# The output projection of a chunk in two halves of eight heads, and the last four heads of the last chunk as a chain by halves of tokens

## The chip, the core and the metric

The kernel runs on one core of a Trainium2 chip. The core has a matrix engine (TensorE, PE in the profile; its weight loads are shown as PEld), a vector engine (VectorE, DVE), an activation engine (ScalarE, ACT), a general engine (GpSimd, POOL) and SyncE (SP), which here only issues transfers. Matmuls write into PSUM, a memory of banks of 512 float32 columns by 128 partitions; VectorE and ScalarE read it from there. The metric is the time of one execution on the device, in microseconds.

## What is computed

Two transformer layers on `x` of 2 sequences by 1024 tokens by 256 features. In each layer attention and feed-forward both read the same normalised input and both are added to the residual. The parts that matter here belong to the second layer:

```python
# _L1_attn_ref: 16 heads of 16 features, rotary positions
attn = jnp.einsum('bhqd,bhkd->bhqk', q, k) * scaling
probs = jax.nn.softmax(attn, axis=-1)
out = jnp.einsum('bhqk,bhkd->bhqd', probs, v)
out = out.transpose(0, 2, 1, 3).reshape(B, S, D)
return out @ out_w.T + out_b
...
xn = _layernorm(x, axis=-1)
x = x + _L1_attn_ref(xn, ...) + _L1_ffn_ref(xn, ...)
return x
```

`out @ out_w.T` is a sum over 256 features, so over 16 heads. It can be cut by heads: the product of the features of heads 0 to 7 with their rows of `out_w.T`, plus that of heads 8 to 15.

## The kernel before

The 2048 tokens are four chunks of 512 (`C`); a chunk is four blocks of 128 tokens (`CT`). `xc[c]` is the residual of chunk `c`, and everything is added into it by VectorE. `parts_left[c]` counts what is still to be added to a chunk: two feed-forward blocks (of 256 tokens, `F`) and the projection. Whoever brings it to zero sends the chunk out.

Layer 0 is ordered by a planner with listed due times (`LEADS`); the change does not touch it. Layer 1 is ordered by hand. Its attention works in eight **units**, each four heads of one sequence: four units for sequence 0, four for sequence 1. A unit has two passes over chunks (`n` = 0, 1), and each pass 8 steps over blocks of 128 keys. The loop at L1332 to L1357 runs over units 0 to 6, 16 steps each. In a step TensorE makes scores for the next unit's maxima (`scm`, read by VectorE's reduction `peak`), scores for this unit's weights (`sce`, read by ScalarE's exponential `pr`), and the weighted sums of the step before (`weigh`, into the bank `po`). The last unit has its own loop (L1360 to L1368) without `scm`.

Between these, TensorE is given **filler** work: a list of generators (the feed-forward blocks of layer 1, `ffn1`, and others). A generator yields the cost of the matmuls it has just issued. `slot` (L1322) shares what is left over the slots left, `left[0] / to_fill[0]`, and lets `fill` (L1216) run the list until that share is spent. In the last unit a slot counts one half. A generator that yields `SOON` has a result on the way which another engine must fetch. There `fill` stops, unless at least 0.85 us (`LEAD`) are still owed; then the next step comes at `go_on(SOON, FIRST)`, in the middle of the next step of the unit, behind the first peak reduction. Units that begin with `heads_of` (L1341) also run an `urgent` list in each slot, whose time is taken off the filler's share.

When a pass has its eighth step, `weigh` copies `po` to `oT` (512 tokens by 4 heads) and asks for `normalise` two slots later (L1131 to L1134). `normalise` transposes `oT` block by block, takes the reciprocal of the sums and multiplies into `att`, the tile of the chunk's 256 features. After the last of the four units of a sequence (`g == NG - 1`, L1151) it queues `project` behind the filler that is running (`queue_next`, L1199). `project` (L1156) transposes all of `att`, four transposes for each half `k` of the features into a bank each, copies one bank by ScalarE and the other by VectorE into `aT`, and then, for each of four token blocks, makes a sum of two products (`mm`), adds it to `xc[c]` and, if this completes the chunk, sends the 128 tokens out. The order of the end (L1369 to L1373) is: the last `weigh`, and then all that is due or left in the filler.

Banks named by `bank(...)` come from one ring of three; `po` has a bank of its own; `sce` and `scm` come from a ring of two pairs. `aT` comes from a ring of three tiles named "stage", which the loads of layer 1's weights also use.

Of the kernel before, what the change touches and what calls it, by code (L numbers as in the profile page):

```python
# [13 lines left out]
F32 = mybir.dt.float32  # L14
# [7 lines left out]
P = 128  # L22
B, S, D = 2, 1024, 256
NH, HD = 16, 16
E = 1024
NB = E // P
C = 512
NC = B * S // C
CT = C // P
BT = S // P  # L30
F = 256
HS = 32
VW = HD + 1
NG = 4
# [5 lines left out]
COL = 4 / 2400  # L40
PASS = 1.1 / 2400
TR = 2 / 2400
# [316 lines left out]
def tile_two_layers(ctx: ExitStack, tc: tile.TileContext, a: dict, out: bass.AP):  # L359
    nc = tc.nc  # L360
    x_d = a["x"].rearrange("(t p) d -> p t d", p=P)
    out_d = out.rearrange("(t p) d -> p t d", p=P)

    state = State()
    tensor, vector, scalar, gpsimd, sync = (
        Engine(state, which, getattr(nc, n))
        for which, n in ((PE, "tensor"), (DVE, "vector"), (ACT, "scalar"), (POOL, "gpsimd"), (None, "sync"))
    )

    def open_pool(stack, name, bufs, grain=1, **kw):  # L370
        return Pool(state, stack.enter_context(tc.tile_pool(name=name, bufs=bufs, **kw)), bufs, grain)

    const = open_pool(ctx, "const", 1)
    small = open_pool(ctx, "small", 4)
    ps = open_pool(ctx, "ps", 1, 2 * C, space=PSUM)
    ident = const.tile([P, P], F32, tag="ident", name="ident")
# [6 lines left out]
    def bank(name):  # L383
        return ps.tile([P, C], F32, tag="bank", name=name, bufs=3)

    po = ps.tile([P, C], F32, tag="po", name="po", bufs=1)
# [16 lines left out]
    def load_w(pool, name, k, n, tag=None):  # L403

        return load(pool, name, a[name].rearrange("(k p) n -> p k n", p=P), [P, k // P, n], tag)
# [6 lines left out]
    xc, xnT = [], []  # L412
# [23 lines left out]
    def mm(out_, pairs):  # L436
        for i, (lhsT, rhs) in enumerate(pairs):
            tensor.matmul(out_, lhsT=lhsT, rhs=rhs, start=(i == 0), stop=(i == len(pairs) - 1))
# [4 lines left out]
    SOON, FIRST, SECOND, LAST, PAIR = 1, 2, 3, 4, 5  # L443
# [102 lines left out]
    def run(gen):  # L546
        for _ in gen:
            pass
# [5 lines left out]
    at = open_pool(ctx, "at", 2)  # L554
# [34 lines left out]
    wo1 = load_w(const, "woT1", D, D)  # L589
# [413 lines left out]
        yield from hadamard_in("wuT1", "wB")  # L1003


    parts_left = [C // F + 1] * NC

    def part_done(c):
        parts_left[c] -= 1
# [16 lines left out]
    units = [(b, g) for b in range(B) for g in range(NG)]  # L1026
# [6 lines left out]
    def later(slots, f):  # L1033
        due.append([slots, f])

    def tick():
        for d in due:
            d[0] -= 1
        ready = [d for d in due if d[0] <= 0]
        due[:] = [d for d in due if d[0] > 0]  # L1040
        for _, f in ready:
            f()
# [76 lines left out]
    att = {}  # L1119

    def weigh(u, n, kt, pr):
        b, g = units[u]
        for h in range(4):
            tensor.matmul(
                po[h * HS : h * HS + VW, :],
                lhsT=va[b, g][:, kt, h, :],
                rhs=pr[h // 2][:, h % 2, :],
                start=(kt == 0),
                stop=(kt == BT - 1),
            )  # L1130
        if kt == BT - 1:  # L1131
            oT = late[0].tile([P, C], F32, tag="oT", name="oT", bufs=1)
            vector.tensor_copy(oT, po)
            later(2, lambda: normalise(u, n, oT))  # L1134

    def normalise(u, n, oT):
        b, g = units[u]
        pt = bank("pt")
        for j in range(CT):
            tensor.transpose(pt[:, j * P : (j + 1) * P], oT[:, j * P : (j + 1) * P], ident)  # L1140
        p4 = pt.rearrange("p (t h s) -> p t h s", t=CT, h=4)
        rz = small.tile([P, CT, 4], F32, tag="rz1", name="rz1")
        vector.reciprocal(rz, p4[:, :, :, HD])
        if g == 0:
            att[b, n] = late[0].tile([P, CT, D], F32, tag="att", name="att")
        vector.tensor_mul(
            att[b, n][:, :, g * 4 * HD : (g + 1) * 4 * HD].rearrange("p t (h d) -> p t h d", h=4),
            p4[:, :, :, 0:HD],
            rz.unsqueeze(3).to_broadcast([P, CT, 4, HD]),
        )  # L1150
        if g == NG - 1:  # L1151
            later(1, lambda: queue_next(project(b, n)))
        left[0] -= CT * P * TR
        spent[0] += CT * P * TR

    def project(b, n):  # L1156

        c = b * (NC // B) + n
        aT = at.tile([P, 2, C], F32, tag="stage", name="aT", bufs=3)
        pts = []  # L1160
        for k in range(2):
            pts.append(bank("pt"))
            for j in range(CT):
                tensor.transpose(pts[k][:, j * P : (j + 1) * P], att[b, n][:, j, k * P : (k + 1) * P], ident)
        yield 2 * CT * P * TR, SOON
        scalar.copy(aT[:, 0, :], pts[0])
        vector.tensor_copy(aT[:, 1, :], pts[1])
        yield 0.0
        parts_left[c] -= 1
        last = parts_left[c] == 0  # L1170
        for j in range(CT):
            py = bank("py")[:, 0:D]
            mm(py, [(aT[:, k, j * P : (j + 1) * P], wo1[:, k, :]) for k in range(2)])
            yield 2 * D * COL, SOON
            vector.tensor_add(xc[c][:, j, :], py, xc[c][:, j, :])
            if last:
                sync.dma_start(out=out_d[:, c * CT + j, :], in_=xc[c][:, j, :])
            yield 0.0

    def search(part):  # L1180

        for i in range(STEPS // 4):
            j = part // 2 * 16 + part % 2 * 2 + i // 2 * 4 + i % 2
            sc = pair("sc")
            plan.burst = True
            burst(scores_of(0, j, sc))
            plan.burst = False
            scores_max(0, j, sc)
            yield
# [9 lines left out]
    def queue_next(gen):  # L1199

        filler.insert(1, gen) if filler else filler.append(gen)

    def step(queue, k=0):
        if callable(queue[0]):
            background.append(queue.pop(0)())
            return
        try:
            x = next(queue[0])
        except StopIteration:
            queue.pop(0)  # L1210
            return
        waits[queue[0]] = x[1] if isinstance(x, tuple) else 0
        spent[k] += cost_of(x)
        left[0] -= cost_of(x)
# [31 lines left out]
    def force(queue):  # L1246
        while queue:
            if queue is background:
                run(queue.pop(0))
            else:  # L1250
                step(queue)
# [16 lines left out]
    halves = norm_halves(xc[0], xnT[0])  # L1268
# [51 lines left out]
    pending = []  # L1320
# [8 lines left out]
    def keep(u, i, prs):  # L1329
        pending.append((u, i // 16, i % 16 // 2, prs))  # L1330
# [28 lines left out]
    u = len(units) - 1  # L1359
    for i in range(0, STEPS, 2):  # L1360
        scs = [pair("sce") for _ in range(2)]
        burst([x for p in range(2) for x in weights_of(u, i, p, scs[p])])
        prs = [weights_exp(sc) for sc in scs]
        go_on(SOON, FIRST)
        while pending:
            weigh(*pending.pop(0))
        slot(0.5)
        keep(u, i, prs)  # L1368
    while pending:  # L1369
        weigh(*pending.pop(0))  # L1370
    while due or filler:
        tick()
        force(filler)  # L1373


def _constants():
# [64 lines left out]
```

## Time and profile before

| | us |
|---|---|
| three runs | 898.34, 898.73, 900.73 (median 898.73) |
| the profiled execution | 900.66 |
| its span, first to last instruction | 898.9 |
| granted TensorE clock, mean | 0.996 of full |
| first half of the program, layer 0 and the first maxima | up to about 203 |
| units 0 to 6 | to about 836 |
| last unit | to 888.9 |
| from the end of `po` to the end | 888.9 to 898.9 |

A row of the timeline gives the start in us, the duration in us, the engine, the operation, the tile written and the tiles read, the shapes, how many instructions are merged, and in brackets how long the engine was idle before and who ended that. All rows have line 316, where a helper issues them, so one goes by tile names. A float32 matmul of the program shows as two rows, and a transpose as one. A matmul's end is modelled, so the start of the next reader is the better mark. The costliest groups that the change's neighbours belong to:

| group | rows | mean ns | engine |
|---|---|---|---|
| `pr<-sce` 128x1024, exponential | 256 | 1023 | ACT |
| `peak<-scm`, reduction | 224 | 1223 | DVE |
| `x<-py` 128x256, add from PSUM | 64 | 419 | DVE |
| `oT<-po` 128x512, copy | 16 | 686 | DVE |
| `aT<-pt` 128x512, copy | 4 | 586 | ACT |
| `aT<-pt` 128x512, copy | 4 | 689 | DVE |
| `va<-pkv` 128x256, copy from PSUM | 16 | 367 | ACT |
| `va<-pqkv` 128x128, add from PSUM | 32 | 281 | DVE |
| `rz<-pt` 128x16, reciprocal | 16 | 250 | DVE |

`out` is written in 16 transfers of 128 KB, with 1.7 us from issue to landing as the median.

### The profile page before, as it was taken

The numbers are of one execution on the slowest core, as the hardware profiler recorded it, in microseconds if no ns is written. First come the engines' busy times: TensorE is split into PE (matmuls) and PEld (weight loads), VectorE is DVE, ScalarE is ACT, GpSimd is POOL, SyncE is SP. The second block draws the span as 40 slices with busy tenths as digits, with TensorE's granted clock in tenths as the row PEclk, the third lists the DMA queues.
The fourth block names the chain that finished last, engine by engine and source line by source line (L and its number), as shares of the span: only waits on it lengthen the run. The fifth ranks groups of instructions, "written<-read, shape, count | busy, mean of one in ns | idle before, by whom it ended". The sixth has DMA issues, their size and how long they took to land.

```text
span 898.9 us, 14598 instructions
## 1 busy us (share of the span) xinstructions
PE 864.9 (96%) x6064; PEld 518.0 (58%) x6064; DVE 583.0 (65%) x956; ACT 438.4 (49%) x641; POOL 212.6 (24%) x280
## 2 busy tenths in 40 slices
PE   8999999989999989999999999999999999999997
PEld 5699866675566434555555555555555555555533
DVE  5887567887677785656865656677565655656211
ACT  6646464515566443445544444455444444444563
POOL 2656877404452140015300000153000000000000
PEclk9999999999999999999999999999999999999999
DMA  9200000000010110000000000000000000000001
GB/s 308 76 1 1 1 1 1 1 1 1 2 48 1 47 47 1 1 1 1 1 1 1 1 1 24 1 1 2 24 1 1 1 1 1 1 1 1 1 7 41
DMA packets 11313, 14.77 MB, mean 16 GB/s; under 512 B 1264, under 2 KB 8944, under 8 KB 11248
## 3 DMA queue, kind: packets, MB, share of 16 engines
q1 hardware_dynamic: 11248, 13.85, 4.6%
q8 instruction: 47, 0.77, 0.4%
q14 instruction: 18, 0.15, 0.1%
HBM read 11.75 MB, written 2.10 MB: 15 GB/s over the span
## 4 chain that ended last, share of the span: by engine, by line
PE 72%; DVE 22%; ACT 3%; issue 2%; DMA 1%; POOL 0%; SPq 0%; ACTq 0%; DVEq 0%
PE pug L316 19%; DVE peak L316 17%; PE scm L316 16%; PE py L316 13%; PE sce L316 7%; PE pqkv L316 5%; PE pt L316 4%; PE pw L316 2%; PE po L316 2%; PE pkv L316 1%; PE sc L316 1%; PE pq L316 1%; ACT pr L316 1%; DVE att L316 1%; DVE t_wgT L316 1%
## 5 line engine op out<-in xcount | busy, mean ns | idle before, releaser
L316 ACT ACTIVATE pr<-sce 128x1024 f32<-128x1024 f32 x256 | 260.2, 1023 | 269.4 <-PE sce L316 269.0
L316 DVE TENSOR_REDUCE peak<-scm 128x2 f32<-128x1024 f32 x224 | 274.0, 1223 | 167.7 <-PE scm L316 167.0
L316 PE MATMUL po<-pr,va 128*17 128x512 f32 x1024 | 135.6, 598 | 0.0
L316 PEld LDWEIGHTS scm<-qk_hi 32*128 32x128 f32 x448 | 41.5, 182 | 151.1 <-DVE peak L316 113.6
L316 PE MATMUL sce<-qk_hi 32*128 32x512 f32 x512 | 123.0, 495 | 4.8 <-DVE peak L316 2.4
L316 PE MATMUL scm<-qk_hi 32*128 32x512 f32 x448 | 111.8, 495 | 11.7 <-DVE peak L316 1.0
L316 POOL CAST tops<-nm 128x16 fp32r<-128x16 f32 x16 | 3.4, 211 | 404.8 <-DVE nm L316 402.3
L316 PE MATMUL sce<-mx,ones_r 32*128 32x512 f32 x512 | 97.3, 392 | 0.1
L316 PE MATMUL sce<-ql,qk_hi 32*128 32x512 f32 x512 | 97.3, 393 | 0.0
L316 PE MATMUL scm<-qk_hi,ql 32*128 32x512 f32 x448 | 89.1, 394 | 0.0
L316 DVE SCALAR_TENSOR_TENSOR act<-act,pug 128x256 f32<-128x256 f32 (+1 forms) x112 | 50.6, 453 | 45.1 <-ACT act L316 38.3
L316 PE MATMUL pug<-xnT,eff_wgT 128*128 128x256 f32 x256 | 69.2, 392 | 0.0
L316 PE MATMUL pug<-xnT,eff_wuT 128*128 128x256 f32 x256 | 68.3, 382 | 0.0
L316 PE MATMUL py<-wd,hid 128*128 128x256 f32 x256 | 63.2, 388 | 0.0
L316 POOL TENSOR_TENSOR hid<-act,hid 128x256 fp32r<-128x256 f32 (+1 forms) x48 | 44.6, 932 | 54.9 <-ACT hid L316 36.0
L316 ACT ACTIVATE act<-pug,ws_ug 128x256 f32<-128x256 f32 x64 | 30.3, 474 | 55.5 <-PE pug L316 55.5
L316 PEld LDWEIGHTS pug<-xnT,eff_wgT 128*128 128x128 f32 x256 | 45.5, 189 | 16.6 <-issue 10.7
L316 PEld LDWEIGHTS py<-wd,hid 128*128 128x128 f32 x256 | 46.4, 190 | 14.8 <-issue 8.5
L316 PEld LDWEIGHTS sce<-qk_hi 32*128 32x128 f32 x512 | 45.9, 182 | 15.4 <-ACT pr L316 9.5
L316 PEld LDWEIGHTS pug<-xnT,eff_wuT 128*128 128x128 f32 x256 | 47.9, 190 | 9.8 <-issue 2.6
L316 PEld LDWEIGHTS sce<-mx,ones_r 32*128 32x128 f32 x512 | 46.6, 183 | 11.0 <-ACT mx L316 0.5
L316 PE MATMUL pqkv<-wqkvT,xnT 128*128 128x384 f32 x128 | 49.6, 506 | 1.6 <-DVE ql L316 1.6
(146 smaller groups left out, 1312.7 us busy)
## 6 DMA issues: line engine op xcount, KB each, us to landing
out<-x SPq DMA_DIRECT2D x16, 128.0 KB, 1.7
x<-in_x SPq DMA_DIRECT2D x3, 512.0 KB, 9.4
both<-in_wuT SPq DMA_DIRECT2D x1, 1024.0 KB, 8.8
both<-in_wgT SPq DMA_DIRECT2D x1, 1024.0 KB, 10.4
wdT<-in_wdT SPq DMA_DIRECT2D x1, 1024.0 KB, 12.6
raw<-in_wdT SPq DMA_DIRECT2D x2, 512.0 KB, 4.3
raw<-in_wgT SPq DMA_DIRECT2D x2, 512.0 KB, 3.7
raw<-in_wuT SPq DMA_DIRECT2D x2, 512.0 KB, 3.3
```

The lines of the kernel that those rows point to most:

```text
L316: return call(*map(real, args), **{k: real(v) for k, v in kw.items()})
```

## The change

`project` takes a half `k`: its four transposes into one bank, one copy (ScalarE for `k` = 0, VectorE for `k` = 1), four products of one matmul each, and four adds. It is queued after every second unit of a sequence (`g % 2`), so the first eight heads are added to the residual two units before the last eight. `parts_left` starts at 4, and a half reports to `part_done`, which sends a finished chunk out in one transfer of 512 KB.

The last pass of the last unit calls the new function `finish` in place of the copy to `oT` and all that followed from it. It handles tokens 0 to 255 and 256 to 511 of the chunk as two halves `h`: `oT` is copied by VectorE for the first half and by ScalarE for the second; each half has its own bank of two transposes, its own reciprocal and multiply, two transposes of the last eight heads' features, and a copy by ScalarE. Then each block of 128 tokens has its product with the last eight heads' rows of the weights, its add and its transfer.

At the end of the program the order of the two loops is turned round: first all that is due or left in the filler, then the last `weigh`, which calls `finish`.

```diff
@@ -1003,7 +1003,7 @@
-    parts_left = [C // F + 1] * NC
+    parts_left = [C // F + 2] * NC
@@ -1130,6 +1130,9 @@
         if kt == BT - 1:
             oT = late[0].tile([P, C], F32, tag="oT", name="oT", bufs=1)
+            if (u, n) == (len(units) - 1, 1):
+                finish(oT)
+                return
             vector.tensor_copy(oT, po)
             later(2, lambda: normalise(u, n, oT))
@@ -1148,34 +1151,62 @@
-        if g == NG - 1:
-            later(1, lambda: queue_next(project(b, n)))
+        if g % 2:
+            later(1, lambda: queue_next(project(b, n, g // 2)))
...
-    def project(b, n):
+    def project(b, n, k):
         c = b * (NC // B) + n
-        aT = at.tile([P, 2, C], F32, tag="stage", name="aT", bufs=3)
-        pts = []
-        for k in range(2):
-            pts.append(bank("pt"))
-            for j in range(CT):
-                tensor.transpose(pts[k][:, j * P : (j + 1) * P], att[b, n][:, j, k * P : (k + 1) * P], ident)
-        yield 2 * CT * P * TR, SOON
-        scalar.copy(aT[:, 0, :], pts[0])
-        vector.tensor_copy(aT[:, 1, :], pts[1])
+        aT = at.tile([P, 2, C], F32, tag="stage", name="aT", bufs=3)[:, 0, :]
+        pt = bank("pt")
+        for j in range(CT):
+            tensor.transpose(pt[:, j * P : (j + 1) * P], att[b, n][:, j, k * P : (k + 1) * P], ident)
+        yield CT * P * TR, SOON
+        (vector.tensor_copy if k else scalar.copy)(aT, pt)
         yield 0.0
-        parts_left[c] -= 1
-        last = parts_left[c] == 0
         for j in range(CT):
             py = bank("py")[:, 0:D]
-            mm(py, [(aT[:, k, j * P : (j + 1) * P], wo1[:, k, :]) for k in range(2)])
-            yield 2 * D * COL, SOON
+            mm(py, [(aT[:, j * P : (j + 1) * P], wo1[:, k, :])])
+            yield D * COL, SOON
             vector.tensor_add(xc[c][:, j, :], py, xc[c][:, j, :])
-            if last:
-                sync.dma_start(out=out_d[:, c * CT + j, :], in_=xc[c][:, j, :])
             yield 0.0
+        part_done(c)
+
+    def finish(oT):
+
+        b, g = units[-1]
+        at0, c = att[b, 1], NC - 1
+        halves = [slice(h * F, (h + 1) * F) for h in range(2)]
+        for h, cols in enumerate(halves):
+            (scalar.copy if h else vector.tensor_copy)(oT[:, cols], po[:, cols])
+        rz = small.tile([P, CT, 4], F32, tag="rz1", name="rz1")
+        aT = at.tile([P, 2, C], F32, tag="stage", name="aT", bufs=3)[:, 0, :]
+        pts = []
+        for h in range(2):
+            pts.append(bank("pt"))
+            for j in range(2):
+                tensor.transpose(pts[h][:, j * P : (j + 1) * P], oT[:, (2 * h + j) * P : (2 * h + j + 1) * P], ident)
+        for h in range(2):
+            p4 = pts[h][:, 0:F].rearrange("p (t h s) -> p t h s", t=2, h=4)
+            two = slice(2 * h, 2 * h + 2)
+            vector.reciprocal(rz[:, two, :], p4[:, :, :, HD])
+            vector.tensor_mul(
+                at0[:, two, g * 4 * HD : (g + 1) * 4 * HD].rearrange("p t (h d) -> p t h d", h=4),
+                p4[:, :, :, 0:HD],
+                rz[:, two, :].unsqueeze(3).to_broadcast([P, 2, 4, HD]),
+            )
+        for h, cols in enumerate(halves):
+            pt = bank("pt")
+            for j in range(2):
+                tensor.transpose(pt[:, j * P : (j + 1) * P], at0[:, 2 * h + j, P : 2 * P], ident)
+            scalar.copy(aT[:, cols], pt[:, 0:F])
+        for j in range(CT):
+            py = bank("py")[:, 0:D]
+            mm(py, [(aT[:, j * P : (j + 1) * P], wo1[:, 1, :])])
+            vector.tensor_add(xc[c][:, j, :], py, xc[c][:, j, :])
+            sync.dma_start(out=out_d[:, c * CT + j, :], in_=xc[c][:, j, :])
@@ -1366,11 +1397,11 @@
-    while pending:
-        weigh(*pending.pop(0))
     while due or filler:
         tick()
         force(filler)
+    while pending:
+        weigh(*pending.pop(0))
```

## The prediction

> **What bounds the kernel now.** I read first the busy shares and the chain of waits, then the timeline of the last 45 us, then the timeline around the two places where a chunk is projected today.
>
> ```profile
> PE 864.9 (96%) x6064; PEld 518.0 (58%) x6064; DVE 583.0 (65%) x956; ACT 438.4 (49%) x641; POOL 212.6 (24%) x280
> PE 72%; DVE 22%; ACT 3%; issue 2%; DMA 1%; POOL 0%; SPq 0%; ACTq 0%; DVEq 0%
> ```
>
> TensorE carries the chain. The change adds no matmul columns and no transposes, so it can only move the time in which TensorE waits. It waits long in one place, the end:
>
> ```profile
> 888.86 0.69 DVE L316 COPY oT<-po 128x512 f32<-128x512 f32 x1 [9.32 <-PE po L316]
> 889.61 0.66 PE L316 MATMUL pt<-ident,oT 128*128 128x128 f32 x4 [0.80 <-DVE oT L316]
> 890.30 0.26 DVE L316 RECIPROCAL rz<-pt 128x16 f32<-128x16 f32 x1 [0.75 <-PE pt L316]
> 890.59 0.42 DVE L316 TENSOR_TENSOR att<-pt,rz 128x256 f32<-128x256 f32 x1
> 891.07 0.66 PE L316 MATMUL pt<-ident,att 128*128 128x128 f32 x4 [0.38 <-DVE att L316]
> 891.77 0.69 DVE L316 COPY aT<-pt 128x512 f32<-128x512 f32 x1 [0.75 <-PE pt L316]
> 892.51 3.29 PE L316 MATMUL py<-woT,aT 128*128 128x256 f32 x14 [0.35 <-DVE aT L316]
> 895.84 0.42 DVE L316 TENSOR_TENSOR x<-py,x 128x256 f32<-128x256 f32 x1 [0.44 <-PE py L316]
> ```
>
> Each row starts where the row above ends: a chain with no cover, 7.4 us from the end of `po` to the end of the last add, and 2.6 us more for the last write (896.26 to 898.9).
>
> In the last unit ACT and the scores hold each other up, and filler work of TensorE is nearly free there up to a point:
>
> ```profile
> 865.88 1.94 ACT L316 ACTIVATE pr<-sce 128x1024 f32<-128x1024 f32 x2 [0.90 <-PE sce L316]
> 868.72 1.94 ACT L316 ACTIVATE pr<-sce 128x1024 f32<-128x1024 f32 x2 [0.90 <-PE sce L316]
> 873.33 1.94 ACT L316 ACTIVATE pr<-sce 128x1024 f32<-128x1024 f32 x2 [2.19 <-PE sce L316]
> 877.13 1.94 ACT L316 ACTIVATE pr<-sce 128x1024 f32<-128x1024 f32 x2 [1.87 <-PE sce L316]
> 880.10 1.94 ACT L316 ACTIVATE pr<-sce 128x1024 f32<-128x1024 f32 x2 [1.03 <-PE sce L316]
> 882.94 1.94 ACT L316 ACTIVATE pr<-sce 128x1024 f32<-128x1024 f32 x2 [0.90 <-PE sce L316]
> ```
>
> A step takes 2.84 us with no filler (865.88 to 868.72), 2.97 with 0.85 us of it (877.13 to 880.10), 3.80 with 1.71 (873.33 to 877.13). So some 0.75 us per step costs nothing and the rest costs its length.
>
> **The tail, part by part.** Counted from 888.86, where `po` is done.
> - The copy of `oT` in halves. A 128x512 DVE copy takes 0.69, a 128x256 DVE read of PSUM 0.42 (`x<-py`), ACT's 0.37 (`va<-pkv`). Both halves lie in the one bank of `po`. The rows on two engines reading one bank:
>
> ```profile
> 27.08 0.39 ACT L316 COPY va<-pkv 128x256 f32<-128x256 f32 x1
> 27.50 0.42 DVE L316 TENSOR_TENSOR kc<-pkv,kvb 128x256 f32<-128x256 f32 x1 [1.80 <-ACT va L316]
> ```
>
>  The two take disjoint columns and neither needs the other, yet DVE waits for ACT. The Trainium skill (PSUM — Partial Sum Buffer, "PSUM bank collisions raise a hardware error") says why: two engines may not touch one bank and partition quadrant at once, reads included, so software has to put them in order. Taken as parallel, both halves are there at 0.42; by row and rule the second is there at 0.42 + 0.03 + 0.37 = 0.82, later than the single copy's 0.69. I take 0.82. It is covered: only the first half is on the chain, and the second is wanted by DVE at 1.55 (below), its transposes at 0.88 + 0.48 = 1.36.
> - First half: copy to 0.42; 0.06 to TensorE; two transposes 0.48 (four took 0.69 up to the reciprocal, each 0.107); reciprocal 0.25 + 0.03; multiply of 128x128 0.28 (`va<-pqkv` of that size); 0.06; two transposes 0.49; ACT copy 0.37. Sum 2.44.
> - Second half: DVE goes on at 1.55: 0.25 + 0.03 + 0.28 + 0.06 = 2.17, then two transposes. TensorE runs in order, so the first product waits for these: 2.17 + 0.32 = 2.49.
> - Products: before, 16 matmul rows of 0.215; now 8, since the first eight heads were added earlier. From the first product to its add is 0.74 (892.51 to 893.25): 3.23. Four adds at 0.42 + 0.03, which is as fast as TensorE makes them (two rows, 0.43): the last ends at 3.23 + 4 x 0.45 = 5.03. The three banks suffice, each is released by the add before.
> - The last write is unchanged: four 128 KB writes on SP's queue, 0.33 of issue each, under the 0.45 between adds.
>
> 7.40 becomes about 5.0: **2.4 us gained**, 1.9 if the halves are not told apart, 2.7 at best.
>
> **The last unit's steps.** Counted by starts of the paired exponentials, 836.97 to 885.78 are 15 steps and 48.8 us, against 15 x 2.84 = 42.6: 6.2 over. The work on TensorE up to this unit is fixed by the budget (what is left over what slots are left), which the change leaves alone. But two first halves (4 transposes of 0.107 and 8 rows of 0.215: 2.1 us each, chunks 2 and 3) are then already done, so 4.3 us more of the last feed-forward block fall into this unit, and the projection of chunk 2 here is 2.1 instead of 4.3: 2.1 us more in all, which is what left the tail. The first six steps stay as they are (20.4 us, 3.3 over). The 4.3 us fill about four steps that were empty at 0.32 over each (the mean of the five from 841.54 to 857.35): 1.35. The half projection in three steps: about 0.6, against 2.9 for the whole one. Sum 5.3: **0.9 gained**, from 0.5 lost to 2.5 gained.
>
> **The first halves in the main loop.** Here TensorE is the bound, and only the waits count. What the row of today's projection shows:
>
> ```profile
> 540.07 1.02 ACT L316 ACTIVATE pr<-sce 128x1024 f32<-128x1024 f32 x1 [1.05 <-PE sce L316]
> 540.50 1.04 PE L316 MATMUL pt<-ident,att 128*128 128x128 f32 x8
> 541.13 0.58 ACT L316 COPY aT<-pt 128x512 f32<-128x512 f32 x1
> 541.57 0.69 DVE L316 COPY aT<-pt 128x512 f32<-128x512 f32 x1 [0.27 <-PE pt L316]
> 541.77 1.25 PE L316 MATMUL py<-woT,aT 128*128 128x256 f32 x4 [0.24 <-ACT aT L316]
> ```
>
> The second four transposes run beside the copy of the first four; TensorE idles 0.24, then 0.25 for DVE's copy: 0.49. A half has nothing beside its copy. The Trainium skill (Perfetto Trace Analysis, "Matmuls") asks for independent matmul groups to rotate through banks so that the evacuation of one overlaps the next; the change takes that away. If rotation were kept, two halves would cost today's 0.49; by the rows one half costs this: begun at the head of a slot its transposes end 0.6 after the slot's start, but ACT is in its exponential until 1.13 and DVE in the peak reduction until 1.0; copy 0.59 or 0.69 and 0.06: product at 1.78, **1.2 of waiting**. Begun late in a slot, with ACT and DVE free: the copy alone, 0.7. If the slot's budget breaks it off after the transposes: nothing, since scores and `po` lie between (so at 638.8, where both copies ran beside the scores and the products began at 639.88 without a wait). Behind the waiting product stand the rest of the slot and then the next scores, so DVE and ACT wait too: the wait counts in full.
>
> A full slot holds about 2.3 us by the code's own budget (271 us over 120 slots) and breaks at a SOON step unless 0.85 are still owed. About a third of the feed-forward blocks end by such a break and put the half at the head of the next slot, half of them run on into it late, the rest break: 0.35 x 1.2 + 0.47 x 0.7 = 0.75 for a half. Six halves lie in the main loop. Two (chunks 0 and 1, first half) follow the block that ends at 417, where slots hold 0.43 to 0.85 beside the heads and break almost always: 0.2 together. Chunk 0's second: 0.75. Chunk 1's second, near the heads' end: 0.5. Chunk 2's first follows the block that ends at 749.94, so it begins at the head of the slot at 751.07, where ACT also has to cast `mx` until 752.68: 1.35. Chunk 3's first: 0.75. Sum 3.55, less today's 0.49: **3.1 lost**, between 0.5 gained and 6.7 lost (six at 1.2, less 0.49).
>
> Free edits: DVE gets 16 more adds less the fewer in the tail, some 6.7 us at 0.42; after the first peak reduction DVE idles 0.83 and an add fits (0.50 left at 545.77), so nothing; without that cover 0.42 each, 6.7 in all. Chunks 0 to 2 now leave as one 512 KB write each, long before the end (512 KB loads land in 3.3 to 4.3; chunk 2's goes out about 8 us before the tail's). `aT` shares the ring of three stage tiles with the weights' loads; the last of these is read at 347.7, and the first half of any chunk comes after its `att` at 357.8, so no load waits.
>
> **The sum.** 2.4 + 0.9 - 3.1 = 0.2 gained. The profiled execution took 900.66 (span 898.9 and 1.8 around it) and would take 900.4; the three runs shown have a median of 898.73, 1.9 below it. I put the change on that: about 898.4.
>
> **The rivals.** A measurement of this kernel can tell about 0.3%, 2.7 us, from no change.
> - Waits of the halves decide: nearly all six begin at the head of a slot. 2.4 + 0.9 - 6.7 = -3.4: **902.1**. For it: the block ends at 417, 750 and 804.5 are all followed by a fresh slot. Against: slots beside heads are short. It makes the kernel measurably slower from 6 us of waits on.
> - The budget breaks most halves: waits vanish with today's 0.49: 2.4 + 0.9 + 0.5 = 3.8 gained: **894.9**. For it: 638.8. Against: 540.5, where the slot ran on.
> - The change does not shorten the end as it says: filler is left over when the steps end and now runs ahead of the last `po` with nothing beside it, up to a half projection, 2.1. Then -1.9: **900.6**. Against: today the queue is empty 8 us before the end.
>
> **How the numbers follow.** Forecast 0.48, slow rival 0.25, fast rival 0.20, leftover 0.07. Forecast and leftover lie within 0.3%, save 0.02 of them on the slow side: slower 0.27, same 0.53, faster 0.20. The forecast's own range is 896.0 to 901.4; to leave out no more than 0.2 it goes to 895.2 and 902.2, which takes in about half of each rival.
>
> **What would show it.** In the tail: DVE `oT` 128x256, then ACT `oT` starting after it, eight `py<-woT,aT` rows and 5 us from `po` to the last add. In the last unit: fewer steps of 2.84, none of 4.6 after the first. In the loop: "ACT aT" and "DVE aT" among TensorE's waits, some 3 us in all. If those waits are above 6 or near 0, the forecast is wrong on its main term; a second `oT` copy beside the first refutes the bank argument.

## The result, and the profile after

The changed kernel takes 904.47 us in the median of seven runs (902.66 to 905.48); the kernel before, run beside it, 900.05 (898.34 to 902.95). The ratio is 1.0043, with a 95% interval from 1.0025 to 1.0061: slower by 2.2 to 5.5 us. The profiled executions differ by 3.8 us (spans 902.7 and 898.9) at the same granted clock, 0.996.

The busy shares and the chain of waits of the changed kernel, as the same two lines were shown of before:

```profile
PE 866.3 (96%) x6064; PEld 516.8 (57%) x6064; DVE 588.4 (65%) x973; ACT 439.2 (49%) x644; POOL 212.8 (24%) x280
PE 71%; DVE 23%; ACT 2%; issue 2%; DMA 1%; POOL 0%; SPq 0%; DVEq 0%; ACTq 0%
```

TensorE has the same 6064 matmuls and 1.4 us more busy time. By these figures 2.4 of the 3.8 us is time in which it stands still, and the shares don't say where. The tail of the changed kernel does not have it; this is its timeline from the end of `po` on (start, duration, engine, operation, in brackets the idle time before and its releaser):

```profile
894.87 0.42 DVE L316 COPY oT<-po 128x256 f32<-128x256 f32 x1 [9.63 <-PE po L316]
895.33 0.37 ACT L316 COPY oT<-po 128x256 f32<-128x256 f32 x1 [1.60 <-DVE oT L316]
895.35 0.84 PE L316 MATMUL pt<-ident,oT 128*128 128x128 f32 x4 [0.53 <-DVE oT L316]
895.82 0.21 DVE L316 RECIPROCAL rz<-pt 128x8 f32<-128x8 f32 x1 [0.53 <-PE pt L316]
...
896.41 0.94 PE L316 MATMUL pt<-ident,att 128*128 128x128 f32 x4 [0.23 <-DVE att L316]
896.51 0.29 DVE L316 TENSOR_TENSOR att<-pt,rz 128x128 f32<-128x128 f32 x1
896.89 0.87 ACT L316 COPY aT<-pt 128x256 f32<-128x256 f32 x2 [1.19 <-PE pt L316]
897.31 1.99 PE L316 MATMUL py<-woT,aT 128*128 128x256 f32 x8
898.05 1.72 DVE L316 TENSOR_TENSOR x<-py,x 128x256 f32<-128x256 f32 x4 [1.25 <-PE py L316]
```

The second half of `oT` starts at 895.33, when the first is done, and its releaser is DVE: the two engines took turns at the bank, as forecast. The first product's row starts 2.44 after the first copy, and the last add ends at 899.77, 4.90 after it. Before it was 7.40. Of these 2.5 us 0.3 go to the last write, which ends 2.9 us after the last add (902.7) where it took 2.6 before.

In the last unit the paired exponentials answer to those shown of before:

```profile
866.42 1.94 ACT L316 ACTIVATE pr<-sce 128x1024 f32<-128x1024 f32 x2 [0.90 <-PE sce L316]
870.44 1.94 ACT L316 ACTIVATE pr<-sce 128x1024 f32<-128x1024 f32 x2 [2.09 <-PE sce L316]
873.40 1.94 ACT L316 ACTIVATE pr<-sce 128x1024 f32<-128x1024 f32 x2 [1.01 <-PE sce L316]
876.83 1.94 ACT L316 ACTIVATE pr<-sce 128x1024 f32<-128x1024 f32 x2 [1.50 <-PE sce L316]
879.67 1.94 ACT L316 ACTIVATE pr<-sce 128x1024 f32<-128x1024 f32 x2 [0.90 <-PE sce L316]
```

The step from 866.42 carries eight matmul rows of the last feed-forward block and takes 4.02; the next, with four, 2.96. No step of the unit is longer than 4.02, where before had two of 4.6. Steps of 2.84 there are six in both, but before five of them had no filler at all, and after only two; the other four carry two matmul rows or four transposes (0.43 us), which cost nothing.

The halves that cost something stand in the main loop. This is the timeline of the changed kernel around the second half of chunk 0:

```profile
552.55 1.23 DVE L316 TENSOR_REDUCE peak<-scm 128x2 f32<-128x1024 f32 x1 [0.49 <-PE scm L316]
552.77 0.66 PE L316 MATMUL pt<-ident,att 128*128 128x128 f32 x4
552.88 1.02 ACT L316 ACTIVATE pr<-sce 128x1024 f32<-128x1024 f32 x1 [1.06 <-PE sce L316]
553.69 0.68 DVE L316 COPY aT<-pt 128x512 f32<-128x512 f32 x1
554.43 1.13 PE L316 MATMUL py<-woT,aT 128*128 128x256 f32 x4 [1.00 <-DVE aT L316]
```

The half stands at the head of a slot. Its transposes are through while DVE is still in the peak reduction (to 553.78); the copy comes behind that, and TensorE idles 1.00 for it. In before the bracket at the corresponding place was 0.24, and 0.25 more for the second copy.

To add such waits up over the program I cut both traces into steps, from the start of one step's `po` matmuls to the next, and took off the filler's matmuls at a fixed length for each row (0.107 for a transpose, 0.213 for a 128x256 row). What remains is the step's own work and its waiting. An ordinary step of units 0 to 6 has 3.27 us of it in every kernel here (3.18 where heads are made), so what a step has over that I take for a wait. (In the table and below, "heads" is the making of the next units' queries, keys and values, and `mx` the tile of the next unit's maxima: four transposes, `pt<-ident_r,tops`, and a copy out by ScalarE. A slot without either is a plain slot. A slot "breaks" when `fill` stops in it at a `SOON`.) The steps that differ between the two kernels by more than 0.15:

| step begins (after) | what is in it | over before, us |
|---|---|---|
| 436.8 | chunk 1, first half, with `mx` and heads | 1.45 |
| 443.9 | its last products, normalisation, heads | 0.55 |
| 539.4 | (chunk 0 whole, before only) | -0.62 |
| 550.6 | chunk 0, second half | 1.21 |
| 640.9 | chunk 1, second half | 1.11 |
| 752.4 | chunk 2, first half, with `mx` | 1.38 |
| 758.7 | its last products, normalisation, feed-forward | 0.49 |

Chunk 0's first half (from 415.6) and chunk 3's (810.2) are not in the list: their slots broke after the transposes and nothing waited. With some tenths in other steps the loop waits 6.05 longer, and has 0.85 us more filler done when the last unit begins. The last unit (from its first weighted sums to the last step's) takes 48.65 instead of 49.03, with 1.3 us more filler in it; from there to the end 10.85 instead of 13.06. The program's first 215 us are 0.5 shorter, which nothing in the change explains. (Two traces of one program differ as much: the loop sum of e4 below, whose loop is that of the changed kernel, is 0.35 smaller.) Sum: 6.05 + 0.85 - 0.38 - 2.21 - 0.53 = 3.8.

### The profile page after: what moved, and what is told of

Same layout as the page of the kernel before. It is cut to its first block, busy times and chain, and to the rows that moved or that the text cites. A ratio compares the mean times of both kernels' runs of the same rounds, so it can differ in the third digit from the quotient of the medians.

```text
span 902.7 us, 14605 instructions
## 1 busy us (share of the span) xinstructions
PE 866.3 (96%) x6064; PEld 516.8 (57%) x6064; DVE 588.4 (65%) x973; ACT 439.2 (49%) x644; POOL 212.8 (24%) x280
## 4 chain that ended last, share of the span: by engine, by line
PE 71%; DVE 23%; ACT 2%; issue 2%; DMA 1%; POOL 0%; SPq 0%; DVEq 0%; ACTq 0%
PE pug L316 19%; DVE peak L316 17%; PE scm L316 16%; PE py L316 13%; PE sce L316 7%; PE pqkv L316 5%; PE pt L316 4%; PE pw L316 2%; PE po L316 2%; PE pkv L316 1%; PE sc L316 1%; PE pq L316 1%; DVE att L316 1%; ACT pr L316 1%; DVE t_wgT L316 1%
```

## The experiments

Theory 1: the time is the copy of a half for which TensorE waits inside one slot. Theory 2: it is the number of banks and additions, 16 more of both, with a ring of three banks that all of the filler shares.

One thing is needed to read the runs. Executions of one kernel spread over some 7 us, and most of that goes with the mean granted clock of the run: the 42 runs of before beside the first four experiments have medians of 897.17, 898.71, 900.49 and 901.70 at mean clocks of 1.000, 0.998, 0.996 and 0.994. In the traces each 0.002 is one dip of about 3.4 us at half clock (last section). So the table gives the ratio over all runs, and the medians at equal clock beside it, and the step sums have the dips of the steps at 238 and 333 taken out; "loop" is what the loop's steps wait more than before's.

| kernel | ratio to before, 95% interval | median at clock 0.996, before beside it | loop | last unit | tail |
|---|---|---|---|---|---|
| before | 1 | | 0 | 49.03 | 13.06 |
| after | 1.0043 [1.0025, 1.0061] | 904.75 | +6.05 | 48.65 | 10.85 |
| e1_break | 1.0012 [1.0002, 1.0022] | 901.08, 900.49 | +3.21 | 49.93 | 10.84 |
| e2_pairs | 1.0030 [1.0017, 1.0044] | 902.17, 900.49 | +3.14 | 49.08 | 10.83 |
| e3_last_chunk | 1.0002 [0.9991, 1.0014] | 901.13, 900.49 | +1.16 | 50.33 | 10.87 |
| e4_old_end | 1.0067 [1.0043, 1.0090] | 904.85 (one run), 900.49 | +5.70 | 48.67 | 12.07 |
| e5_early | 1.0034 [1.0018, 1.0050] | 903.25, 900.66 | +4.14 | 49.33 | 10.84 |
| e6_early_pairs | 1.0017 [1.0006, 1.0028] | 902.20, 900.66 | +2.85 | 49.54 | 10.82 |
| e7_more_adds | 1.0013 [0.9999, 1.0026] | 902.27, 900.66 | +1.18 | 49.39 | 13.19 |
| e8_placed | 0.9975 [0.9961, 0.9988] | 899.00, 900.26 | +0.37 | 48.65 | 10.86 |
| e9_placed_pairs | 0.9978 [0.9966, 0.9991] | 898.44, 900.26 | -0.93 | 49.06 | 10.81 |
| e10_copy_twice | 1.0116 [1.0081, 1.0152] | none | +10.92 | 48.64 | 10.85 |

The experiments are written against the changed kernel, e7 against the one before. `...` in a diff stands for lines left out.

**e1_break: the slot always ends after the transposes.**

```diff
-        yield CT * P * TR, SOON
+        yield CT * P * TR, FIRST
```

> The changed kernel, with the slot always ended after the four transposes of a half, so that the copy of aT is put between two peaks and the products come in the next slot, behind scores and po. Theory 1 (the time went into the copy of a half that TensorE waits for inside one slot): the four halves that ran on in their slot lose their waits of 1.45, 1.21, 1.12 and 1.37 us, so the span falls by about 5, from 902.7 to 897 to 898.5, about 1 us below before. Theory 2 (the banks and the doubled additions: 48 products of one matmul pair each instead of 28 with two, a ring of three banks): no change within 0.5, span 902 to 903.

The four waits are gone and half of what they cost came back: the loop falls from 6.05 to 3.21. The eight runs at a clock of 0.996 have a median span of 899.3, above the range of theory 1. What took their place is in the timeline of e1 at the same half:

```profile
550.48 1.23 DVE L316 TENSOR_REDUCE peak<-scm 128x2 f32<-128x1024 f32 x1 [0.50 <-PE scm L316]
550.69 0.66 PE L316 MATMUL pt<-ident,att 128*128 128x128 f32 x4
550.80 1.02 ACT L316 ACTIVATE pr<-sce 128x1024 f32<-128x1024 f32 x1 [1.05 <-PE sce L316]
551.75 0.50 PE L316 MATMUL scm<-qk_hi 32*128 32x512 f32 x2 [0.41 <-DVE peak L316]
```

Four transposes are 0.43 us of filler. Now the next scores wait for the peak of this step, which holds their bank pair until 551.71. The slots from 548.5 and 810.0 had only these 0.43 us of filler and waited 0.5 each for DVE, so by this estimate some 0.9 us of filler are needed to cover the peak. At 638.6 four feed-forward rows stood in the slot ahead of the transposes, and it waited for nothing.

That is 1.0 of what is left. Another 1.05 stands in the two slots with heads in which chunk 1's half and its products lie (435.7 and 441.0), 0.6 at chunk 2's (749.5 and 753.7), and 1.07 in two steps that hold no row of a half at all (614.9 and 621.1). There the feed-forward block comes to a new bank after only two rows of the slot, while `mx` or the normalisation still holds it (waits of 0.28 for ScalarE's copy of `mx`, 0.29 for VectorE's multiplication into `att`). So in these slots the ring of three banks costs 0.5 us, whichever work takes the bank.

**e2_pairs: two token blocks' products in one bank, one addition for both.**

```diff
-        for j in range(CT):
-            py = bank("py")[:, 0:D]
-            mm(py, [(aT[:, j * P : (j + 1) * P], wo1[:, k, :])])
-            yield D * COL, SOON
-            vector.tensor_add(xc[c][:, j, :], py, xc[c][:, j, :])
+        for j in range(0, CT, 2):
+            py = bank("py").rearrange("p (t n) -> p t n", t=2)
+            for t in range(2):
+                mm(py[:, t, :], [(aT[:, (j + t) * P : (j + t + 1) * P], wo1[:, k, :])])
+            yield 2 * D * COL, SOON
+            vector.tensor_add(xc[c][:, j : j + 2, :], py, xc[c][:, j : j + 2, :])
```

> The changed kernel, with the products of two token blocks in one bank and one addition of 128x512 for both in the main loop: half as many banks and half as many additions for the same columns. Theory 1 (the copy of a half): only the two smaller excesses of the slots after a first half (0.55 and 0.50 us) can go, span 901.5 to 902.7. Theory 2 (banks and additions): most of the 6 us goes, span 896.5 to 898.

Neither range: 902.17 at a clock of 0.996 is a span of 900.4, and the loop falls by 2.9. The steps that lost their excess are those at 436.8 (1.45), 443.9 (0.55) and 758.7 (0.49); the other three halves keep theirs (1.20, 1.11 and 1.38). So theory 1 holds for these three, 3.7 us. Of the other 2.5 only the 0.49 is a clean price of banks, since the half stands in the same slots as before. The 2.0 of chunk 1's first half is not: with products of 0.85 instead of 0.43 the first half of chunk 0 was done sooner, and chunk 1's transposes came one slot earlier, where that slot broke.

**e3_last_chunk: halves for the last chunk only.**

```diff
-    parts_left = [C // F + 2] * NC
+    parts_left = [C // F + 1] * (NC - 1) + [C // F + 2]
...
-        if g % 2:
+        if (b, n) == (B - 1, 1) and g % 2:
             later(1, lambda: queue_next(project(b, n, g // 2)))
+        elif g == NG - 1:
+            later(1, lambda: queue_next(project_whole(b, n)))
...
```

`project_whole` has the transposes, copies and products of the old `project`, and `part_done` at its end.

> Only the last chunk is projected in halves, with the chain at the end; chunks 0 to 2 are projected whole, as before. Both theories: the main loop has one half (which broke its slot and waited for nothing) and the three whole projections of before, so up to the last unit it takes what before took, within 0.7; the end keeps its 2.2. Span 896 to 898. If the last unit does not keep its 0.4 (the last chunk's first half puts 2.1 us more filler work there), 898 to 898.7.

A miss: the six runs at a clock of 0.996 have a median span of 899.3, 1.3 above the range, and 0.6 above the one for a last unit that loses its 0.4, which it did (50.33). The tail kept its 2.2. But the one half left in the loop, chunk 3's first, which broke its slot in the changed kernel, ran on in its slot here (1.22 over before in the step from 803.2): the filler ahead of it stood differently. And in the last unit the whole projection of chunk 2 had its ScalarE copy queued behind an exponential of 1.94; TensorE waited 1.58 (bracket of the products at 875.88). So whether a half waits depends on where the filler ends before it, which the change does not control.

**e4_old_end: all halves, but the end as before.**

```diff
-            if (u, n) == (len(units) - 1, 1):
-                finish(oT)
-                return
...
+            if c == NC - 1 and k:
+                sync.dma_start(out=out_d[:, c * CT + j, :], in_=xc[c][:, j, :])
...
```

The two loops at the end of the program also stand in their old order again.

> The changed kernel with all halves, but the end written as before: one copy of po, one transposition of the four heads, one multiplication, and the last half's four transposes, its copy and its products one after the other. The end then gains only what was projected earlier (8 matmuls of 0.215 less, no second aT copy: 1.1 to 1.5) and loses what the chain by halves of tokens brought (the rest of the 2.2): the end 11.7 to 12.2 us instead of 10.9, span 903.5 to 904.

The tail takes 12.07, inside the range. So of the 2.2 us that the change gains there, 1.0 comes from having eight heads done earlier and 1.2 from the chain by halves of tokens.

**e5_early: transposes and copy at the head of a slot, ahead of the filler that stands there; only the products are queued.**

```diff
-            later(1, lambda: queue_next(project(b, n, g // 2)))
+            later(1, lambda: turn(b, n, g // 2))
...
+    def turn(b, n, k):
+        aT = at.tile([P, 2, C], F32, tag="stage", name="aT", bufs=3)[:, 0, :]
+        pt = bank("pt")
+        for j in range(CT):
+            tensor.transpose(pt[:, j * P : (j + 1) * P], att[b, n][:, j, k * P : (k + 1) * P], ident)
+        (vector.tensor_copy if k else scalar.copy)(aT, pt)
+        left[0] -= CT * P * TR
+        spent[0] += CT * P * TR
+        queue_next(project(b, n, k, aT))
...
```

> The changed kernel, with the four transposes of a half and its copy put at the head of the slot after the normalisation, ahead of whatever filler stands there, and only the products queued behind the current block: feed-forward matmuls lie between copy and products. At equal granted clock (each dip of the clock that a run has costs 1.55 to 1.7 us; the profile of the changed kernel had two, mean clock 0.996). Theory 1: no half waits for its copy any more, the four waits of 1.45, 1.21, 1.12 and 1.37 go and nothing takes their place, unlike in e1 where a slot with little filler then waited for the peak: span 897 to 898.5 at 0.996. Theory 2 (banks and additions): the slots still pay for 48 products, span 900.5 or more at 0.996.

Missed by theory 1, and inside theory 2's range: 903.25 at a clock of 0.996 is a span of 901.5. The halves in plain slots cost nothing any more. But chunk 1's two halves now came into the slots that begin a batch of heads. The timeline of e5 at the second of them:

```profile
585.39 1.22 DVE L316 TENSOR_REDUCE peak<-scm 128x2 f32<-128x1024 f32 x1 [0.30 <-PE scm L316]
585.62 0.66 PE L316 MATMUL pt<-ident,att 128*128 128x128 f32 x4
...
586.28 0.28 PE L316 MATMUL pt<-ident,rot 128*128 128x128 f32 x1
...
586.89 0.68 DVE L316 COPY aT<-pt 128x512 f32<-128x512 f32 x1
587.49 0.41 DVE L316 TENSOR_TENSOR ql<-pt,qk_hi 128x256 fp32r<-128x256 f32 x1
587.63 1.56 PE L316 MATMUL pqkv<-wqkvT,xnT 128*128 128x384 f32 x4 [1.01 <-DVE aT L316]
```

The heads' matmul `pqkv` has nothing to do with `aT`; the releaser is the copy because it empties the bank that comes next in the ring. So the shared ring makes the copy count even here: 1.01 in this row, 0.66 at 407.60. The additions, the other part of theory 2, have no share in it: e6, with half as many, has the same 1.23 in that step. The products of both chunks' first halves then met in the step with `mx` (437.0, 1.18), and 0.55 stands in a step without any half (617.9), as in e1.

**e6_early_pairs: e5 with e2's additions.**

> e5 with the products of two token blocks in one bank and one addition of 128x512 for both. If what is left after e5 is the ring of three banks in the slots where mx is made (0.55 and 0.50 in the changed kernel), another 0.5 to 1.0 goes: span 896 to 897.5 at a mean clock of 0.996, about 2 us below before. If e5 has already none of these waits, the same as e5 within 0.3.

1.3 us less in the loop than e5 and 1.05 at equal clock, a little more than the 0.5 to 1.0 expected. The span of 900.4 at 0.996 missed the range, which stood on e5's. The slots of 0.55 and 0.50 that are named there make no `mx`: they hold a normalisation (`pt<-ident,oT`).

**e7_more_adds: the kernel before, each half of a product in its own bank and added by itself.**

```diff
-            py = bank("py")[:, 0:D]
-            mm(py, [(aT[:, k, j * P : (j + 1) * P], wo1[:, k, :]) for k in range(2)])
-            yield 2 * D * COL, SOON
-            vector.tensor_add(xc[c][:, j, :], py, xc[c][:, j, :])
+            for k in range(2):
+                py = bank("py")[:, 0:D]
+                mm(py, [(aT[:, k, j * P : (j + 1) * P], wo1[:, k, :])])
+                yield D * COL, SOON
+                vector.tensor_add(xc[c][:, j, :], py, xc[c][:, j, :])
```

> The kernel before, with each half of a product in a bank of its own and added by itself (16 more banks and additions for four chunks), the transposes and copies still of all sixteen heads at once. This is Theory 2 alone, without any copy of a half. Theory 1: between 0 and 0.6 in the loop, and in the tail up to 0.9 more (four more additions of 0.42 behind products of 0.21 each): span 899 to 900.4 at 0.996. Theory 2: 2 us or more in the loop, span 901 or more.

Between the two: 1.2 in the loop (0.36 to 0.39 in each of three steps) and 0.4 in the last unit, 1.6 at equal clock. A product of before is four matmul rows, 0.85 us, and one of e7 two rows, 0.43 (the 0.21 that the expectation gives is one row). In the first of the three steps two products pass, and the third waits 0.36 (at 544.94) for an addition of 0.42 that stands on VectorE behind the peak reduction. Theory 2 has a price of its own. Its share of the 6.05 can't be read from here, though: eight of e7's sixteen additions lie in the loop, the change puts all its sixteen there, and what they cost depends on the place (e8).

**e8_placed: e5 with the place chosen.** Chunk 1's halves wait ten slots, until the heads are done; the last unit is as in the changed kernel.

```diff
-            later(1, lambda: turn(b, n, g // 2))
+            if u == len(units) - 1:
+                later(1, lambda: queue_next(project(b, n, g // 2)))
+            else:
+                later(10 if n and u < 4 else 1, lambda: turn(b, n, g // 2))
...
```

> e5 with the place of the early transposes chosen: chunk 1's two halves, whose transposes fell into the slots that begin a batch of heads (0.87 and 1.23 lost there), come ten slots later, when the heads are done, and the half of the last unit is left as in the changed kernel. If the losses of e5 were the three banks shared with the heads, they go, and with them the waits at 439 (1.18) and 444 (0.53), where the products of chunk 1's first half met the transposes of mx: e5's 902.4 at a mean clock of 0.996 falls by 3 to 4, to 898.4 to 899.4. If a half costs what it costs wherever it stands, 901 to 902.4.

The loop falls from 4.14 to 0.37, and the kernel is faster than before: 0.9975, interval 0.9961 to 0.9988. Some of that is the clock, 0.9971 in the mean of its runs against 0.9962 beside it; at equal clock it is 1.3 us. Its median of 899.00 at 0.996 is a span of 897.2, below the range. Two excesses of 0.57 and 0.49 are left, one in a step with `mx` (433.0) and one in a step with a normalisation (749.4).

The first of them splits the largest item of the changed kernel, the 1.45 at 436.8. First the rows of the changed kernel there, then the rows of e8 in its step from 433.0:

```profile
439.69 0.65 PE L316 MATMUL py<-woT,aT 128*128 128x256 f32 x2
440.62 0.65 PE L316 MATMUL pt<-ident,att 128*128 128x128 f32 x4 [0.28 <-ACT mx L316]
...
441.94 1.13 PE L316 MATMUL py<-woT,aT 128*128 128x256 f32 x4 [0.68 <-DVE x L316]
```

```profile
435.85 0.65 PE L316 MATMUL py<-woT,aT 128*128 128x256 f32 x2
436.77 1.13 PE L316 MATMUL pug<-xnT,eff_wgT 128*128 128x256 f32 x4 [0.27 <-ACT mx L316]
```

In both the last product of chunk 0 (two rows) takes a bank in the slot with `mx`, and the next work waits 0.28 or 0.27 for the bank that ScalarE's copy of `mx` empties. In e8 this work is a feed-forward block, and the step's excess is 0.57. In the changed kernel it is chunk 1's half. By subtraction some 0.9 of the 1.45 comes with that half. (The brackets show about half of such an excess; the ends of matmuls, from which they are counted, are modelled.)

**e9_placed_pairs: e8 with e2's additions.**

> e8 with two token blocks' products in one bank and one addition for both. The additions and banks that e7 priced at 1.5 us for sixteen go back to the number of before: 0.5 to 1.2 less than e8, span 897 to 898.7 at a mean clock of 0.996, 0.2 to 1.9 below before. If the theory of the two causes is right, this is all that the main loop can give back, and the kernel is a little faster than before.

The loop waits 0.93 less than before's, so the whole projection's own wait of 0.62 is gone as well. At equal clock this is 0.6 below e8 and 1.8 below before (a span of 896.6, 0.4 under the range); over all runs the two can't be told apart (0.9978 and 0.9975). No step of units 0 to 6 waits over 0.15 longer than before's. The timeline of e9 at chunk 0's second half:

```profile
539.03 0.66 PE L316 MATMUL pt<-ident,att 128*128 128x128 f32 x4
539.13 1.02 ACT L316 ACTIVATE pr<-sce 128x1024 f32<-128x1024 f32 x1 [1.05 <-PE sce L316]
539.52 1.46 PE L316 MATMUL py<-wd,hid 128*128 128x256 f32 x6
539.96 0.68 DVE L316 COPY aT<-pt 128x512 f32<-128x512 f32 x1
...
550.76 1.03 PE L316 MATMUL py<-woT,aT 128*128 128x256 f32 x4
```

The same peak, transposes and copy as in the changed kernel, but six matmul rows of a feed-forward block lie behind the transposes, and the products come when that block is done.

The excess of 0.49 shows the price of a bank alone. These are the products and the feed-forward block behind a normalisation in the changed kernel's step from 758.7, and then in e9's from 752.1:

```profile
761.34 1.03 PE L316 MATMUL py<-woT,aT 128*128 128x256 f32 x4
762.62 1.10 PE L316 MATMUL pug<-xnT,eff_wgT 128*128 128x256 f32 x4 [0.26 <-DVE att L316]
```

```profile
754.70 1.03 PE L316 MATMUL py<-woT,aT 128*128 128x256 f32 x4
755.57 1.03 PE L316 MATMUL pug<-xnT,eff_wgT 128*128 128x256 f32 x4
```

The same rows in the same order. With two banks for the two products, the block needs the normalisation's bank and waits until VectorE has multiplied it into `att`; with one bank for both it does not wait. e8, without the pairs, waits 0.25 there.

**e10_copy_twice: the copy of each half in the loop done twice.**

```diff
         (vector.tensor_copy if k else scalar.copy)(aT, pt)
+        (vector.tensor_copy if k else scalar.copy)(aT, pt)
```

> The changed kernel, with the copy of each half in the main loop done twice, one after the other on the same engine into the same tile. Theory 1: where TensorE waits for the copy in the slot (four halves), each second copy of 0.58 or 0.68 counts in full, and where the slot broke (chunk 0's and chunk 3's first half) it counts nothing: 2.3 to 2.8 more, span 905 to 905.5 at a mean clock of 0.996. Theory 2: the copies lie beside other work, at most 0.5 more.

The loop grew by 4.9 where 2.3 to 2.8 were expected. Two places answer as theory 1 says: the step of chunk 1's first half grew by 0.62 (a ScalarE copy is 0.58), that of chunk 1's second by 0.73 (a VectorE copy is 0.68); the halves in broken slots stayed at 0 and 0.2. The other two grew by 2.0 each with the step after, which the copy can't explain. The windows of e10 there (from and to, busy time of PE, PEld, DVE, ACT and POOL, granted clock, transfers):

```profile
552.00:555.00 3.00, 1.28 (x9) 0.84 (x12) 2.12 (x4) 0.53 (x1) 0.00 (x0) 1.00 0.03 5
555.00:558.00 3.00, 3.00 (x18) 0.73 (x18) 1.56 (x2) 1.02 (x1) 0.00 (x0) 0.50 0.00 0
558.00:561.00 3.00, 3.00 (x23) 2.22 (x20) 1.89 (x3) 1.02 (x1) 0.00 (x0) 0.93 0.00 0
561.00:564.00 3.00, 2.90 (x23) 1.19 (x21) 1.27 (x2) 1.45 (x2) 0.00 (x0) 1.00 0.52 175
```

After the wait, the clock is at half for some 3.4 us. And here is the wait that came ahead of it:

```profile
552.32 1.41 DVE L316 COPY aT<-pt 128x512 f32<-128x512 f32 x2
553.78 1.13 PE L316 MATMUL py<-woT,aT 128*128 128x256 f32 x4 [1.72 <-DVE aT L316]
```

Lengthened from 1.00 to 1.72, the wait cost its 0.7 and about 1.3 more by the clock. It happened at both of the two longest waits (1.72 and 1.77), and not at those of 1.29 and 1.58. So this run shows theory 1 where the clock held, and its total of 4.9 must not be read as the price of copies.

## Why the prediction was wrong

The forecast was 898.4, with 902.2 as its upper end and a chance of 0.27 for slower. Its sum was 0.2 gained; the profiled executions show 3.8 lost, the medians 4.4. Another 1.3 us of the miss is its base: the three runs had a median of 898.73, the seven of 900.05. The step that failed is the term for the first halves in the main loop, 3.1 lost: the loop lost 6.05.

- **Tail, 2.4 gained:** right. 2.2, by the rows foretold (2.5 to the last add, less 0.3 for the write, which was put at unchanged): the first product 2.44 after the copy (2.49 was the sum), the last add at 4.90 (5.03), the second `oT` copy serialised and covered. That the three banks suffice was true here.
- **Last unit, 0.9 gained for 2.1 us more filler:** right in kind. 0.4 gained for 1.3 more; the other 0.85 were done in the loop, probably because a slot's share is met in lumps of a generator's step. The steps of 4.6 went, as foretold. The steps of 2.84 did not become fewer, since up to 0.43 us of filler fits into one; the step that the prediction reads as one without filler (865.88 to 868.72) already held four transposes.
- **First halves in the main loop, 3.1 lost: this step failed.** The mechanism, a half with nothing beside its copy, was right; the size was not, and a second cause was put at nothing. The prediction's 3.55 for the halves became 6.2:
  - The first halves of chunks 0 and 1, said to "break almost always: 0.2 together", cost 2.0 (1.45 + 0.55). Chunk 0's transposes broke their slot, as said, and its products took four slots. But the last of these products met the bank of `mx` (in e8 that alone is 0.57), and chunk 1's half, queued behind it, ran on in that slot. A weight was used where the order of the program decides: `fill` runs past `SOON` whenever 0.85 are owed.
  - 0.75 for chunk 0's second half, 0.5 for chunk 1's, 0.75 for chunk 3's, against 1.21, 1.11 and 0: together 2.3 against 2.0. The 1.2 for a half at the head of a slot was right for both that ran on in a plain slot, and 1.35 for chunk 2's with `mx` (1.38). That the three sum so nearly right is luck: none of the three was near its own term.
  - Banks were left out of the loop, and 16 more adds were put at nothing, since DVE has room. DVE has room, but the banks that wait for it have not: 0.49 at 758.7 goes when two products share a bank (e9), and e7 shows 1.2 in the loop for eight more banks and adds without any copy of a half. In before each product gave one add 0.85 of TensorE time to hide in; after, 0.43, no more than the add itself (0.42), which on VectorE also waits behind the peak reduction (1.22).
- Against today's 0.49 the whole projection's wait was 0.62. So the halves come to 5.6 lost instead of 3.1; the rest of the 6.05 is tenths in other steps.
- **The rival "waits of the halves decide"** said 902.1, by six waits of 1.2. The span of 902.7 looks like it, but not its working: four halves waited, two did not, and a part of the loss was the shared banks.

What stays open: how the 0.9 that comes with chunk 1's first half divides between its copy and the banks (its products waited 0.68, for a copy by ScalarE that ended at 441.89 and an addition that ended at 441.95). No run takes one of the two away and leaves the half in its place; e2 and e8 both moved it.

## What to carry to other kernels

Cutting one evacuated product into two makes each copy stand alone: put transposes and copy ahead of filler that is independent of them, and only the products behind it. That alone left the kernel 0.3% slower (e5); with chunk 1's halves also kept out of the slots whose heads use the same banks it went from 0.4% slower to 0.2% faster (e8). Count a shared ring of banks by its slowest reader per bank: if a bank's matmuls become as short as its addition (0.43 and 0.42 us here), the additions are no longer free on an engine that is idle a third of the time. And where a wait depends on where a budget ends, walk the order through for each instance instead of weighting it.

## What the runs showed of the hardware

After some of the longer stretches in which TensorE stood idle the granted clock dropped to half, for 3.41 us each time, and not after every one of the same length. In the twelve traces, idle stretches after 60 us and before the tail give: of 2.24 to 2.26 us (in the step at 333, waiting for `peak`), ten of twelve followed by a dip; 1.72 and 1.77, both; 1.56 and 1.58, three of fourteen; 0.9 to 1.29, none of ten. A dip costs 1.55 to 1.7 us, which is 3.4 at half. This fits most of the spread between runs of one kernel, and e10's mean clock of 0.989 to 0.994 in its four runs against 0.9962 in the mean of before's 43 beside them (its profiled run, at 0.994, has three dips). The Trainium skill (TensorE: Matmul & The Clock Gate, "Part 1: The HAM clock gate (the "warmup" mystery)") has the length, a free-running window of about 3.4 us, which agrees with these dips and would explain the chance in them; its rule to avoid idle gaps above about 3.4 us ("HAM oscillation — how this bites in real kernels") is too wide for this kernel, where gaps of 1.6 to 2.3 already did it. By that rule e10's waits would have cost only their own length; by these rows a wait of 1.0 cost its own length, and the two of 1.7 some 3 us each.
